# A graph network on one core: edge products copied into the gather ring, and gathers that accumulate onto them

## The chip, the cores and the metric

The kernel runs on one core of one Trainium2 chip. The metric is device time in microseconds (us), the median of several runs. Before the change it is 4117.99 us (three runs, 4102.45 to 4145.95). A profile is one further execution, taken by the hardware profiler.

## What is computed

There are 6250 nodes with 256 features and 100,000 edges with 64 features, sorted by their target `dst`; `src` is random. Two layers follow one another, and each ends in a residual sum and a layer norm:

```python
# layer 0
e = relu((x[dst] - x[src]) @ theta_w.T + theta_b + x[src] @ phi_w.T + phi_b)
x = layernorm(x + segment_max(e, dst))            # 0 where a node has no edge
# layer 1
hv = x @ W_in + b_in
for W, b in ((W_u0, b_u0), (W_u1, b_u1)):
    m = relu(concat([hv[src], he]) @ W + b)       # he: the 64 edge features
    hv = where(has_in, segment_max(m, dst) + hv, hv)
x = layernorm(x + relu(hv @ W_ro + b_ro))
```

So there are three passes over the edges, each a maximum over the edges of a node. Since a product with a row of a table can be taken before the rows are gathered, an edge costs a gathered row of a table of 6250 x 256 numbers; in passes 1 and 2 the product of its own 64 features is added to that row.

## The kernel before

The edges lie in 782 steps of 128 (one on each partition), the steps in 17 blocks: twelve of 56 steps, then 48, 32, 16, 8 and 6. Within a block each partition holds consecutive edges, one a step. Eight steps make a chunk (98 in all). `sweep(r)` (L705) issues one pass in program order; nothing reorders it, each engine takes its instructions as they stand there and waits on semaphores.

For a step `s` the loop at L906 does this:

- `sources` (L716) issues on POOL the indirect gather of step `s + 16` (`AHEAD`): 128 rows of 1 KB of `table[r]`, by the indices `s_s`, into a tile `run` of 8 steps, of which there are 4 (`bufs=4`).
- In passes 1 and 2, `features` (L723) loads a chunk of transposed edge features `hT` from the ACT queue, three chunks early, and `pair` (L727) makes on PE the product `hp` of two steps in one PSUM bank; there are two such banks (`tag="he"`). L923 adds it to the two gathered steps on DVE.
- L926 is the running maximum on DVE: `cur = max(min(prev, lim), cur)`, where `lim` cuts it at a new node.
- After each chunk L932 stores the 1 MB tile to `S` in DRAM from SP's queue.

At the end of a block `over_lanes` (L734) carries the maximum across partitions: PE transposes the last step (`lp`), DVE scans it (`scan`, L746, at the first step after the block), PE turns it back (`back`, L753, one step later), ACT copies it to `cs`.

`node` (L763) finishes 128 nodes, 49 tiles of them in a pass. Its parts are put on steps with `at(slot, f)`. `rows` (L769) gathers on POOL, at step `g`, the last edge's row of each node from `S`; it waits for all stores issued before it. `picks` and `carried` (three and two steps before `b`) bring the carried part `v` into PSUM. From step `b` on comes the arithmetic: `first_a` to `first_i` in pass 0 (relu, residual with `x_sb`, statistics on DVE, square root on ACT, norm, transposes on PE, two products with `wcat`, the next table's rows stored from ACT's queue), `next_a` to `next_d` in pass 1, `next_a` to `next_c` and `last_d` to `last_g` in pass 2. The planner at L896 to L901 sets the steps:

```python
gap = (4, 4, 6)[r]
...
    e = max(FIRST[SPAN[t][1]] + BLOCKS[SPAN[t][1]], begin)
    b = max(b + (gap if b < FS else 3), e + 4, min(e + AHEAD + 4, FS + 4))
    node(t, max(e, b - AHEAD - 4), b)
```

`e` is the end of the last block in which the tile's nodes can end. In pass 0 there are also the counts of edges per node (`count`, L643), from which `end_i`, the indices for `rows`, come, and `theta` (L797), the part of layer 0 that belongs to the target. `x` lies in SBUF (`x_sb`, 49 KB a partition); layer 0's result takes its place there.

Of the kernel before, what the change touches and what calls it, by code (L numbers as in the profile page):

```python
# [17 lines left out]
P = 128  # L18
N = 6250
D = 256  # L20
# [22 lines left out]
KEPT = 7  # L43
# [11 lines left out]
SPAN = [span(t) for t in range(NT)]  # L55

# [377 lines left out]
def gnn_kernel(  # L434
# [6 lines left out]
    table = [dram.tile([ROWS, D], F32, name=f"table{r}") for r in range(3)]  # L441


    jmp = const.tile([P, P], I32)
# [7 lines left out]
    col_i = const.tile([P, P], I32)  # L452
# [97 lines left out]
def in_order(ctx: ExitStack, tc: tile.TileContext, g):  # L550
# [9 lines left out]
    heT, xTn, xn, out = (g[n] for n in ("heT", "xTn", "xn", "out"))  # L560
    ctx.enter_context(tc.manual_schedule())
# [4 lines left out]
    x_sb = one.tile([P, NT, D], F32, name="x_sb")  # L566
# [9 lines left out]
    def weight(w, name):  # L576
        t = one.tile([P, 2, D], F32, name=name)
        nc.scalar.dma_start(t, w.rearrange("(k p) f -> p k f", p=P))
        return t
# [7 lines left out]
    tb, pb = line(g["th_b"], "tb"), line(g["ph_b"], "pb")  # L587
    wcat = one.tile([P, 2, 2 * D], F32, name="wcat")
    nc.scalar.dma_start(wcat[:, :, :D], g["w_in"].rearrange("(k p) f -> p k f", p=P))
    winT = weight(g["w_inT"], "winT")  # L590
    wu0 = weight(g["w_u0"][:D, :], "wu0")
# [51 lines left out]
    def count(c):  # L643
        k = min(K, FS - c * K)
        cut = slice(c * K, c * K + k)
        ol = work.tile([P, K, P], BF16, name="ol", bufs=1)
# [57 lines left out]

    def sweep(r):  # L705
# [10 lines left out]
        def sources(s):  # L716
            if s % K == 0:
                runs[s // K] = work.tile([P, K, D], F32, name="run", bufs=4)
            nc.gpsimd.indirect_dma_start(  # L719
                out=runs[s // K][:, s % K, :], out_offset=None, in_=table[r],  # L720
                in_offset=bass.IndirectOffsetOnAxis(ap=s_s[:, s:s + 1], axis=0))

        def features(c):  # L723
            hT[c] = work.tile([P, K // 2, P], F32, name="hT", bufs=4)
            nc.scalar.dma_start(hT[c].rearrange("p q e -> p (q e)"), heT[c])

        def pair(i):  # L727
            c, q = divmod(i, K // 2)
            hp[i] = psum.tile([P, 512], F32, tag="he", name="hp")
            nc.tensor.matmul(hp[i], hT[c][:, q, :], whe[r - 1].rearrange("p s f -> p (s f)"), start=True, stop=True)  # L730
            if q == K // 2 - 1:
                del hT[c]

        def over_lanes(b, last):  # L734
# [25 lines left out]
            at(FIRST[b] + BLOCKS[b], scan)  # L760
            at(FIRST[b] + BLOCKS[b] + 1, back)

        def node(t, g, b):  # L763
# [22 lines left out]
            def carried():  # L786
                assert max(carried_in) - SPAN[t][0] < KEPT
                o["v"] = psum.tile([P, 512], F32, tag="v", name="v")
                for blk, p in o["pick"]:
                    nc.tensor.matmul(o["v"][:, :N1], p, cs[:, blk % KEPT, :N1], start=(blk == SPAN[t][0]),  # L790
                                     stop=(blk == SPAN[t][1]))

            def x_in():
                o["xT"] = work.tile([P, 2, P], F32, name="xT", bufs=3)
                nc.sync.dma_start(o["xT"], xTn[:, :, t * P:(t + 1) * P])
# [12 lines left out]
            def first_b():  # L808
                nc.vector.tensor_add(o["m"], o["m"], h_sb[:, t, :])
                nc.scalar.activation(o["m"], o["m"], AF.Relu, scale=has[:, t:t + 1])  # L810

            def first_c():
                nc.vector.tensor_add(o["m"], o["m"], x_sb[:, t, :])
# [4 lines left out]
            def first_e():  # L818
                norm(x_sb[:, t, :], o["m"], *o["mv"])
                o["aT"] = turned(x_sb[:, t, :])  # L820

            def first_f():
                o["g"] = times(o["aT"], wcat[:, :, D:], b2, D)

            def first_g():
                o["ps"] = times(o["aT"], wcat[:, :, :D], None, D)

            def first_h():
                new = work.tile([P, D], F32, name="new", bufs=3)
                nc.scalar.copy(new, o["g"][:, :D])  # L830
                nc.scalar.dma_start(table[1][t * P:(t + 1) * P, :], new)

            def first_i():
                nc.scalar.copy(h_sb[:, t, :], o["ps"][:, :D])

            def next_a():
                nc.vector.tensor_max(o["m"], o["m"], o["v"][:, :D])  # L837
                nc.scalar.activation(o["m"], o["m"], AF.Relu, scale=has[:, t:t + 1])
# [8 lines left out]
            def next_d():  # L847
                new = work.tile([P, D], F32, name="new", bufs=3)
# [3 lines left out]
            def last_d():  # L852
                nc.vector.scalar_tensor_tensor(o["m"], o["ps"][:, :D], 0.0, x_sb[:, t, :], OP.max, OP.add)  # L853

            def last_e():
                o["mv"] = stats(o["m"], "m")

            def last_f():
                o["y"] = work.tile([P, D], F32, name="new", bufs=3)
                norm(o["y"], o["m"], *o["mv"])  # L860
# [4 lines left out]
            at(g, rows)  # L865
            if r == 0:
# [3 lines left out]
            at(b - 3, picks)  # L870
            at(b - 2, carried)
            if r == 0:
                for i, f in ((0, first_a), (1, first_b), (3, first_c), (4, first_d), (6, first_e), (7, first_f),
                             (8, first_g), (9, first_h), (10, first_i)):
                    at(b + i, f)
            else:
                for i, f in ((0, next_a), (2, next_b), (3, next_c)):
                    at(b + i, f)
                for i, f in ((5, next_d),) if r == 1 else ((5, last_d), (6, last_e), (8, last_f), (9, last_g)):
# [3 lines left out]
        if r == 0:  # L883
# [4 lines left out]
            for i in range(NT // PART):  # L888
                at(14 + 8 * i, lambda i=i: nc.sync.dma_start(x_sb[:, i * PART:(i + 1) * PART, :],
                                                             xn[:, i * PART:(i + 1) * PART, :]))  # L890
# [5 lines left out]
        gap = (4, 4, 6)[r]  # L896
# [95 lines left out]
```

## Time and profile before

| | |
|---|---|
| median of three runs | 4117.99 us |
| profiled execution | 4091.96 us |
| its span | 4090.2 us |
| mean granted TensorE clock | 0.667 of full |
| first to last gather, passes 0, 1, 2 | 59.8 to 1339.3, 1389.9 to 2664.5, 2710.4 to 4007.4 us |
| read from and written to HBM | 401.01 MB, 333.16 MB |

In the lines of groups a row has source line, engine, operation, what it writes and reads, count, busy time and mean ns of one, then the engine's idle time before it and who ended that. In the answers by stretches the columns are the length, then busy time and number of instructions of PE, its weight loads, DVE, ACT and POOL, then the granted TensorE clock, the mean busy share of the 16 DMA engines and GB/s. A timeline line has the start, the duration, the instruction, and in brackets the idle time before it with its releaser. Releasers are inferred from semaphore events, and some matmul records can be missing.

### The profile page before, as it was taken

To read this page: it belongs to the slowest core of one execution; us is meant where nothing else is said; L and a number is where in the kernel's file an instruction comes from. 1 tells how busy PE (TensorE), PEld (TensorE's weight loads), DVE (VectorE), ACT (ScalarE), POOL (GpSimd) and SP (SyncE) were. 2 spreads that over 40 slices of the span, in tenths; PEclk is the share of its full clock that TensorE was granted. 3 is DMA by queue.
4 is the path that set the end of the run, shared out by engine and by line. 5 is a ranking of instruction groups with operands and counts; after the bars stand their busy time and mean duration, and the time that the engine had idled before them with its cause. 6 is when DMAs were issued, how large, how long until landed. Compare 5 with 4: busy or idle time off the path is not lost.

```text
span 4090.2 us, 22048 instructions
## 1 busy us (share of the span) xinstructions
PE 2032.6 (50%) x4957; PEld 915.2 (22%) x4957; DVE 2083.0 (51%) x4526; ACT 280.7 (7%) x770; POOL 2459.6 (60%) x2499
## 2 busy tenths in 40 slices
PE   5433444232334745455464555664455545555557
PEld 4222222111112311111121222221121212122223
DVE  2766733433334555454554454545555555555555
ACT  1000010000101100000000000110000000000001
POOL 3777755666664466566666655546666666655542
PEclk7555565555555867676777777786766777777766
DMA  6755544454554456565555555545655555555542
GB/s 223 250 195 181 195 157 169 166 181 161 170 168 147 147 189 211 172 205 179 195 192 184 181 181 183 172 164 191 204 191 193 191 180 192 182 174 171 175 146 86
DMA packets 237763, 735.87 MB, mean 180 GB/s; under 512 B 51880, under 2 KB 91799, under 8 KB 200375
## 3 DMA queue, kind: packets, MB, share of 16 engines
q0 software_dynamic: 119664, 326.92, 26.7%
q1 hardware_dynamic: 66096, 334.71, 21.5%
q10 hardware_dynamic: 51862, 72.75, 5.4%
q8 instruction: 42, 0.69, 0.1%
q14 instruction: 99, 0.80, 0.1%
HBM read 401.01 MB, written 333.16 MB: 179 GB/s over the span
## 4 chain that ended last, share of the span: by engine, by line
another core or an unknown queue 31%; DVE 18%; PE 16%; issue 15%; POOL 9%; DMA 8%; ACT 1%; ACTq 0%; DVEq 0%; POOLq 0%; SPq 0%
POOL run L719 9%; DVE run L926 8%; DVE run L923 7%; DMA run<-table,s_s 5%; PE hp L730 5%; PE prod L700 4%; PE prod L702 2%; PE v L790 2%; DMA S<-run 1%; PE ps L533 1%; PE tp L692 1%; ACT aT L694 1%; DVE pick L783 1%; DMA hT<-in_heT 0%
## 5 line engine op out<-in xcount | busy, mean ns | idle before, releaser
L719 POOL DMA_INDIRECT run<-table,s_s x2346 | 2316.6, 987 | 1294.2 <-issue 696.2
L730 PE MATMUL hp<-whe,hT 128*128 128x512 f32 x1564 | 1054.5, 779 | 589.7 <-DVE run L923 378.2
L926 DVE SCALAR_TENSOR_TENSOR run<-run,lim 128x256 f32<-128x256 f32 x2295 | 1110.6, 484 | 205.7 <-DMA run<-table,s_s 120.5
L923 DVE TENSOR_TENSOR run<-run,hp 128x512 f32<-128x512 f32 x782 | 533.7, 682 | 809.0 <-remote 459.7
L730 PEld LDWEIGHTS hp<-whe,hT 128*128 128x128 f32 x1564 | 308.0, 233 | 1190.7 <-DVE run L923 699.6
L771 POOL DMA_INDIRECT m<-S,end_i x147 | 142.4, 969 | 291.6 <-DMA S<-run 191.4
L700 PE MATMUL prod<-wcat,aT 128*128 128x256 f32 x392 | 160.4, 550 | 261.9 <-ACT aT L694 167.6
L790 PE MATMUL v<-cs,pick 128*128 128x256 f32 (+1 forms) x468 | 192.6, 540 | 123.9 <-DVE pick L783 70.9
L692 PE MATMUL tp<-ident,h_sb 128*128 128x128 f32 x196 | 52.7, 361 | 358.9 <-DVE h_sb L841 223.6
L653 PE MATMUL hist<-oh,ol 128*128 128x49 bf16 x782 | 48.8, 217 | 249.2 <-DVE oh L650 182.2
L700 PEld LDWEIGHTS prod<-wcat,aT 128*128 128x128 f32 x392 | 95.5, 268 | 314.2 <-ACT aT L694 177.6
L790 PEld LDWEIGHTS v<-cs,pick 128*128 128x128 f32 x468 | 116.2, 272 | 199.6 <-issue 83.5
L746 DVE TENSOR_TENSOR_SCAN cT<-lim,cT,lp 128x128 f32<-128x128 f32 x96 | 40.8, 468 | 218.5 <-PE lp L741 144.5
L853 DVE SCALAR_TENSOR_TENSOR m<-prod,x_sb 128x256 f32<-128x256 f32 x49 | 20.8, 424 | 248.9 <-remote 169.9
L700 PE MATMUL prod<-wro,aT 128*128 128x256 f32 x196 | 90.4, 609 | 96.8 <-issue 76.1
L647 DVE TENSOR_TENSOR ol<-col,lo 128x1024 bf16<-128x1024 bf16 x98 | 119.3, 1217 | 26.3 <-remote 25.7
L692 PEld LDWEIGHTS tp<-ident,h_sb 128*128 128x128 f32 x196 | 25.1, 173 | 451.4 <-issue 318.5
L741 PE MATMUL lp<-ident,run 128*128 128x128 f32 x102 | 28.7, 375 | 183.0 <-ACT lim L739 101.5
L700 PE MATMUL prod<-wu,aT 128*128 128x256 f32 x196 | 75.6, 524 | 68.4 <-ACT aT L694 36.7
L837 DVE TENSOR_TENSOR m<-m,v 128x256 f32<-128x256 f32 x98 | 40.5, 414 | 134.9 <-remote 78.1
L653 PEld LDWEIGHTS <-ol 128*128 128x128 bf16 x782 | 42.8, 117 | 276.2 <-DVE ol L647 164.5
L700 PE MATMUL prod<-th,xT 128*128 128x256 f32 x196 | 95.5, 640 | 8.8 <-issue 8.8
(116 smaller groups left out, 1326.0 us busy)
## 6 DMA issues: line engine op xcount, KB each, us to landing
S<-run SPq DMA_DIRECT2D x291, 1024.0 KB
hT<-in_heT ACTq DMA_DIRECT2D x196, 256.0 KB
run<-table,s_s POOLq DMA_INDIRECT x2346
table<-new ACTq DMA_DIRECT2D x98, 128.0 KB
xg<-in_xTn SPq DMA_DIRECT2D x7, 896.0 KB
table<-g SPq DMA_DIRECT2D x7, 896.0 KB
xT<-in_xTn SPq DMA_DIRECT2D x49, 128.0 KB
x_sb<-in_xn SPq DMA_DIRECT2D x7, 896.0 KB
```

What stands on the lines that cost most here:

```text
L533: nc.tensor.matmul(ps[:, q * D:(q + 1) * D], xg[:, k, (i + q) * P:(i + q + 1) * P], wd[:, k, :], start=(k == 0), stop=(k == 1))
L647: nc.vector.tensor_tensor(ol[:, :k, :], col.unsqueeze(1).to_broadcast([P, k, P]), lo[:, cut].unsqueeze(2).to_broadcast([P, k, P]), OP.is_e ...
L653: nc.tensor.matmul(hist[:, :NT], ol[:, j, :], oh[:, j, :], start=(c == 0 and j == 0), stop=(c == NG - 1 and j == k - 1))
L692: nc.tensor.transpose(tp[:, k * P:(k + 1) * P], a[:, k * P:(k + 1) * P], ident)
L700: nc.tensor.matmul(ps[:, :n], aT[:, k, :], w[:, k, :], start=(k == 0), stop=(k == 1 and b is None))
L702: nc.tensor.matmul(ps[:, :n], every[0:1, :], b, start=False, stop=True)
L719: nc.gpsimd.indirect_dma_start(out=runs[s // K][:, s % K, :], out_offset=None, in_=table[r], in_offset=bass.IndirectOffsetOnAxis(ap=s_s[:, ...
L730: nc.tensor.matmul(hp[i], hT[c][:, q, :], whe[r - 1].rearrange("p s f -> p (s f)"), start=True, stop=True)
L771: i = nc.gpsimd.indirect_dma_start(out=o["m"], out_offset=None, in_=S_r[:P * (FIRST[SPAN[t][1]] + BLOCKS[SPAN[t][1]]), :], in_offset=bass. ...
L790: nc.tensor.matmul(o["v"][:, :N1], p, cs[:, blk % KEPT, :N1], start=(blk == SPAN[t][0]), stop=(blk == SPAN[t][1]))
L923: nc.vector.tensor_add(two, two, hp.pop(s // 2))
L926: nc.vector.scalar_tensor_tensor(cur, prev, lim[:, s:s + 1], cur, OP.min, OP.max)
```

## The change

The edge products no longer meet the gathered rows on DVE. The ring of `run` tiles grows from 4 to 10 and is shared by the passes. For a chunk of passes 1 and 2, `products` loads `hT` (from SP's queue), makes the four products on PE and lets ACT copy each from PSUM into the ring tile; it is called seven chunks (56 steps) ahead of the step, and for the first seven chunks of a pass during the last four chunks of the pass before. The gather into that tile then has `compute_op` add. Steps ahead for the gathers stay 16.

To make room, `x_sb` goes: rows of `x` are loaded for each tile in pass 0 and rows of layer 0's result, stored to `x1` in DRAM, in pass 2. Some weights that are needed early lie in a tile of the ring. Also: `scan` and `back` run 15 steps later (5 near the end), `v` is copied to SBUF by ACT 17 steps before its use, relu of the nodes moves from ACT to DVE (in the last step of pass 2 the other way), two products with `wcat` become one of 512 columns, and nodes are at least 6 steps apart in all passes.

```diff
-KEPT = 7
+RING = 10
+EARLY = 7
+KEPT = 9
+def calm(s):
+    return 16 if s < FS - 120 else 6
...
+    def products(r, c):
+        hT = work.tile([P, K // 2, P], F32, tag="pt", name="hT", bufs=4)
+        nc.sync.dma_start(hT.rearrange("p q e -> p (q e)"), heT[c])
+        runs[r, c] = work.tile([P, K, D], F32, tag="run", name="run", bufs=RING)
+        for q in range(min(K, FS - c * K) // 2):
+            hp = psum.tile([P, 512], F32, tag="he", name="hp")
+            nc.tensor.matmul(hp, hT[:, q, :], whe[r - 1].rearrange("p s f -> p (s f)"), start=True, stop=True)
+            nc.scalar.copy(runs[r, c][:, 2 * q:2 * q + 2, :].rearrange("p s f -> p (s f)"), hp)
...
             nc.gpsimd.indirect_dma_start(
-                out=runs[s // K][:, s % K, :], out_offset=None, in_=table[r],
-                in_offset=bass.IndirectOffsetOnAxis(ap=s_s[:, s:s + 1], axis=0))
+                out=runs[r, c][:, j, :], out_offset=None, in_=table[r],
+                in_offset=bass.IndirectOffsetOnAxis(ap=s_s[:, s:s + 1], axis=0),
+                **({"compute_op": OP.add} if r > 0 else {}))
...
-            at(FIRST[b] + BLOCKS[b], scan)
-            at(FIRST[b] + BLOCKS[b] + 1, back)
+            e = FIRST[b] + BLOCKS[b]
+            at(e + calm(e) - 1, scan)
+            at(e + calm(e), back)
...
+                o["v"] = work.tile([P, D + 2], F32, name="vs", bufs=4)
+                nc.scalar.copy(o["v"][:, :N1], v[:, :N1])
+            def x_row():
+                o["x"] = work.tile([P, D], F32, name="x", bufs=3)
+                nc.sync.dma_start(o["x"], xn[:, t, :] if r == 0 else x1[t * P:(t + 1) * P, :])
...
-                nc.scalar.activation(o["m"], o["m"], AF.Relu, scale=has[:, t:t + 1])
+                nc.vector.tensor_scalar(o["m"], o["m"], 0.0, has[:, t:t + 1], OP.max, OP.mult)
...
-                norm(x_sb[:, t, :], o["m"], *o["mv"])
-                o["aT"] = turned(x_sb[:, t, :])
+                norm(o["x"], o["m"], *o["mv"])
+                o["aT"] = turned(o["x"])
+                nc.scalar.dma_start(x1[t * P:(t + 1) * P, :], o["x"])
...
-            at(b - 3, picks)
-            at(b - 2, carried)
+            at(b - late - 2, picks)
+            at(b - late - 1, carried)
...
-        gap = (4, 4, 6)[r]
+        gap = 6
...
-            b = max(b + (gap if b < FS else 3), e + 4, min(e + AHEAD + 4, FS + 4))
-            node(t, max(e, b - AHEAD - 4), b)
+            c = calm(e)
+            b = max(b + (gap if b < FS else 3), min(max(e + 2 * c + 4, e + AHEAD + 4), FS + 4))
+            node(t, max(e, b - AHEAD - 4), b, c)
...
-                if s % 2 == 0:
-                    if s + 2 < FS:
-                        pair(s // 2 + 1)
-                    two = runs[c][:, j:j + 2, :].rearrange("p s f -> p (s f)")
-                    nc.vector.tensor_add(two, two, hp.pop(s // 2))
-            cur = runs[c][:, j, :]
+            if j == 0:
+                if r > 0 and c + EARLY < NG:
+                    products(r, c + EARLY)
+                elif r < 2 and c >= NG - 4:
+                    for i in range(2 * (c - NG + 4), min(2 * (c - NG + 5), EARLY)):
+                        products(r + 1, i)
+            cur = runs[r, c][:, j, :]
```

## Prediction, on record before the change was measured

> **What bounds the kernel now.** I read the page first, then busy time by stretches, the timeline of one stretch, and the waits of POOL. The stretches are cut at the first and last gather of each pass; between them lie the lead-in, the turn to the next pass (passes 0 to 1: 50.6 us, 1 to 2: 45.9 us) and the tail.
>
> ```profile
> PE 2032.6 (50%) x4957; PEld 915.2 (22%) x4957; DVE 2083.0 (51%) x4526; ACT 280.7 (7%) x770; POOL 2459.6 (60%) x2499
> q0 software_dynamic: 119664, 326.92, 26.7%
> q1 hardware_dynamic: 66096, 334.71, 21.5%
> q10 hardware_dynamic: 51862, 72.75, 5.4%
> another core or an unknown queue 31%; DVE 18%; PE 16%; issue 15%; POOL 9%; DMA 8%; ACT 1%; ACTq 0%; DVEq 0%; POOLq 0%; SPq 0%
> L719 POOL DMA_INDIRECT run<-table,s_s x2346 | 2316.6, 987 | 1294.2 <-issue 696.2
> L926 DVE SCALAR_TENSOR_TENSOR run<-run,lim 128x256 f32<-128x256 f32 x2295 | 1110.6, 484 | 205.7 <-DMA run<-table,s_s 120.5
> L923 DVE TENSOR_TENSOR run<-run,hp 128x512 f32<-128x512 f32 x782 | 533.7, 682 | 809.0 <-remote 459.7
> ```
>
> No engine is full on this page, and nearly a third of the chain has no name. The stretches (POOL is the last engine column) give the floor:
>
> ```profile
> 59.80:1339.30 1279.50, 467.77 (x1777) 280.70 (x1778) 624.63 (x1383) 103.72 (x296) 845.02 (x827) 0.54 0.53 179
> 1389.90:2664.50 1274.60, 684.88 (x1297) 252.69 (x1297) 658.21 (x1317) 62.19 (x164) 801.90 (x826) 0.72 0.57 188
> 2710.40:4007.40 1297.00, 701.52 (x1267) 263.35 (x1268) 698.41 (x1488) 56.66 (x157) 797.05 (x825) 0.71 0.55 184
> ```
>
> POOL's timeline shows 0.30 us between any two gathers, so an issue costs 1.25 us, not 0.95. Busy time plus 0.30 per instruction makes 1093 of 1279.5 us in pass 0, 1050 of 1274.6 in pass 1, 1045 of 1297.0 in pass 2. What POOL stands still is 186, 225 and 252 us: 663 us, the most that can be won while a gather costs POOL what it does.
>
> Why it stands still is on DVE's timeline, in pass 1:
>
> ```profile
> 1443.99 0.69 DVE L923 TENSOR_TENSOR run<-run,hp 128x512 f32<-128x512 f32 x1 [3.87 <-issue]
> 1448.90 0.69 DVE L923 TENSOR_TENSOR run<-run,hp 128x512 f32<-128x512 f32 x1 [3.18 <-DMA run<-table,s_s]
> 1454.49 0.69 DVE L923 TENSOR_TENSOR run<-run,hp 128x512 f32<-128x512 f32 x1 [3.86 <-remote]
> ...
> 1511.92 0.68 DVE L923 TENSOR_TENSOR run<-run,hp 128x512 f32<-128x512 f32 x1
> 1513.56 0.68 DVE L923 TENSOR_TENSOR run<-run,hp 128x512 f32<-128x512 f32 x1
> ```
>
> The adds of two steps come 5.5 us apart (10 in 55.3 us, granted clock 0.50), then 1.64 us apart (clock 1.00). The three releasers named for the slow ones differ, and none can be true: by 1494.6 us POOL had issued 80 gathers and DVE had made 27 adds, 54 steps, so the rows lay there 26 steps ahead. What is late is the edge product, whose matmul records end too early or are missing. Run back to back at speed, a product takes PE 1.37 us (four in 5.46 us at 1505.06). So in slow stretches PE gives a product per 5.5 us, 2.8 us a step, more than twice POOL's pace; DVE has only the two PSUM buffers as stock; the ring of 4 chunks fills, and POOL stops:
>
> ```profile
> POOL run L719 <- DVE run L926: 77.4, 15, 14.9
> POOL run L719 <- DMA S<-run: 76.1, 10, 13.9
> POOL run L719 <- DVE run L923: 31.3, 8, 11.0
> ```
>
> Two of its halts: 3.64 us before 1484.67, 11.61 before 1506.11. Pass 0 has no edge products, but DVE waits there for transposes of the lanes (cT from lp: 135.4 us in 11 waits) and for picks (no: 93.7 and 49.6 us), PE again.
>
> **What the skill says.** "TensorE: Matmul & The Clock Gate", Part 1: an idle array falls to half clock after a window of some 3.4 us and comes back after a busy one; a caveat reports it stuck at a quarter for 50 us and more. The trace agrees with the caveat in size: 5.5 against 1.37 us is a factor of 4, at a recorded 0.50. "DMA: Bandwidth & Descriptors", SWDGE vs HWDGE: accumulating is for GpSimd's software path only, and one copy is a pair of descriptors; Rules for kernel authors: the accumulate reads its destination and writes it later. It gives no price, and no accumulating gather is in this trace. "ScalarE: Activation LUTs", What ACT_TABLE_LOAD costs: 186 ns + 0.833 ns per element for an instruction with immediates, 612 ns for 512; the trace has 586 ns for such a copy (g from ps, L536), which I use.
>
> **The change part by part.**
>
> *Adds off DVE.* 391 x 0.682 = 267 us a pass leave DVE; its scan, 0.484 us a step, then needs 379 us of a pass. DVE follows the rows and no longer sets the pace: no time by itself, but a DVE held up by late products is what filled the ring.
>
> *Products into the ring.* PE makes the same 391 products a pass. ACT gets 391 x 0.586 = 229 us a pass, and 49 copies of v at about 0.37 us = 18 us; it has 62 and 57 us of busy time now, so it has room. Its order does not: copies of products lie ahead of node work, and with PE at 5.5 us a product, the four of a chunk hold ACT 22 us. Pass 0 has no products, and in pass 1 the node's DVE work takes nothing late from ACT; in pass 2 the norm waits for the square root two steps (2.5 us) after its statistics. Cover gone, DVE stalls there, and rows waits with it; I leave 5 us for it beyond pass 1.
>
> *Slack.* Each gather of passes 1 and 2 now waits for its copy; behind it in POOL's queue stand all later gathers and the rows gathers, and DVE waits for both. PE may now be 56 steps ahead of DVE; gathers are issued up to 16, so some 40 steps are stock. In a slow stretch PE loses 1/1.25 - 1/2.8 = 0.44 step per us, so the stock lasts about 90 us, against 55 and 40 us of the two slow stretches that I read (1443.9 to 1499.2, 1544 to 1584); at speed it gains about 1/0.69 - 1/1.25 = 0.65, less the node matmuls. Most halts should be covered, not all: node matmuls slow down as well, and PE works in bursts that may let the clock fall oftener. I leave 105 of 225 us in pass 1, 110 of 252 in pass 2.
>
> *Lanes and nodes.* Moving scan and back 15 steps later (5 near the end) and v 17 steps ahead, into SBUF, takes DVE's waits for lp and v away: 135 + 94 + 50 us of DVE in pass 0. POOL meets them only through the rows gathers and the ring (its waits there: m for S 88 us, run for lp 34 and for DVE 27). I halve its 186: 93 stay. A ring of 10 chunks is part of this. The gap of 6 slots instead of 4 puts one node more behind the last step (7 for 6) in passes 0 and 1: under 5 us.
>
> *Moved DMAs.* 196 loads of hT go from ACT's queue to SP's, 7 chunks early; SP waits there for stores in order, which follow DVE, so they have 60 us of cover. x rows: 49 loads of 128 KB for 7 of 896 KB, the same bytes; x1 adds 49 stores on ACT (0.33 us each) and 49 loads in pass 2: 12.8 MB of 736. Nothing. Relu on DVE (0.42 for ACT's 0.51), one 512-wide product for two: nothing.
>
> *The accumulating gather.* The unknown. POOL: below nothing is excluded, since it does all it does now; zero is the low end. High end: a third descriptor for two, half of 0.97 us again. I take 0.05 us, for the extra wait on ACT's copies: 782 x 0.05 = 39 us a pass. DMA: a gather takes 26.7% x 4090.2 / 2493 = 0.44 us of each of the 16 engines, the rest (26.9% over 2346 steps) 0.47 a step. Doubled (read two, write one) a step needs 1.35 us of engine time, and the busiest stretch shown runs at 0.89. That is at POOL's pace; [...] I take it as just covered.
>
> *Sum, on the profiled span.* Lead-in 60 + pass 0 (1093 + 93 = 1186) + turn 51 + pass 1 (1050 + 39 + 105 = 1194) + turn 46 + pass 2 (1045 + 39 + 110 = 1194) + tail 83 = 3814 us against 4090. The profiled execution took 4091.96 us, 26 below the median 4117.99; so 3840 for the median.
>
> **Rivals.**
>
> (a) *POOL pays for the accumulate* (slower). With 0.48 us more an issue, a pass is 1050 + 375 + 20 = 1445; in all 4316, median 4342. It decides from about 0.05 + 276/1564 = 0.23 us an issue, a little later since longer issues also give PE time. For: software writes the descriptors. Against: 0.95 us may be mostly fixed. 0.14.
>
> (b) *DMA saturates* (slower). At three times the engine time a step needs 1.79 us: 1400 us a pass at full share; with POOL's other stalls none, 3 x as above gives about 4225, median 4250, more at 0.89. Breaks even near 2.2 to 2.5 times. For: 0.89 is already seen. Against: the mean is 0.55. 0.13.
>
> (c) *Slow PE remains the bound.* Bursts keep it slow; the stock only delays halts. Passes 1 and 2 keep 200 us each of stillness, 185 more than in my sum: 4025 in the median. For: the clock stood at 0.50 in each stretch of 10 us from 1440 to 1500, under steady demand. Against: the halts of POOL come only when a stock of 2 products is gone. 0.20, of which three quarters are still over 1% below before.
>
> (d) *All halts go.* Pass 1093, 1060, 1060: 3453 with the rest, median 3480 to 3600. 0.08.
>
> Mine: 0.45, own range 3620 to 3960. Together faster by over 1% (under 4077) 0.68, within 1%, about what a measurement here can tell, 0.05, slower 0.27. The range 3540 to 4370 leaves out half of (d) and the far ends of (a) and (b).
>
> **What would show it.** Right: L719 at about 1.0 us and 0.30 gap in passes 1 and 2, POOL still 210 us there together, ACT near 300 us a pass, no DVE wait of 3 us on products. (a): L719 over 1.2 us. (b): DMA share near 0.9 in passes 1 and 2, POOL waiting for landings. (c): POOL waits for ACT's copies, clock 0.50 in long stretches. The forecast fails if a gather's price rises by over 0.2 us, or if PE's slow stretches outlast 90 us or halts come back as soon as they end.

## The result, and the profile after

The changed kernel takes 4552.82 us (median of 4 runs, 4535.99 to 4555.76), the kernel before beside it 4110.22 (4095.35 to 4145.95): 1.105 times, interval 1.098 to 1.113. It is slower; the forecast was 3840, with 4370 as the upper end of its range. Where the runs of one kernel spread, a ratio here uses those within 1.5% of its fastest.

From the page of the changed kernel: busy time of the engines, the queue of the gathers, the gather (now L744), the scan (L946) and ACT's copy of a product (L727):

```profile
PE 2037.2 (45%) x4761; PEld 925.5 (20%) x4761; DVE 1643.8 (36%) x3891; ACT 723.5 (16%) x1601; POOL 3391.2 (74%) x2499
q0 software_dynamic: 269808, 326.92, 40.6%
L744 POOL DMA_INDIRECT run<-table,s_s x2346 | 3244.0, 1383 | 854.4 <-issue 632.4
L946 DVE SCALAR_TENSOR_TENSOR run<-run,lim 128x256 f32<-128x256 f32 x2295 | 1107.7, 483 | 2259.6 <-DMA run<-table,s_s 2043.9
L727 ACT COPY run<-hp 128x512 f32<-128x512 f32 x782 | 458.6, 586 | 2126.5 <-PE hp L726 1938.3
```

DVE lost its 439 us and ACT gained its 443, as planned; POOL gained 932 us with the same 2499 instructions. The mean gather went from 987 to 1383 ns, although the 782 gathers of pass 0 are unchanged. Queue q0 moves the same 326.92 MB in 269808 packets instead of 119664. DVE now waits 2044 us for rows.

The same three stretches as before (columns: from and to, length, PE, weight loads, DVE, ACT, POOL, granted clock, DMA share, GB/s):

```profile
58.70:1361.00 1302.30, 468.55 (x1612) 236.29 (x1613) 628.36 (x1405) 99.97 (x293) 850.50 (x825) 0.55 0.54 179
1444.20:2953.60 1509.40, 707.15 (x1310) 295.82 (x1309) 437.70 (x988) 279.77 (x557) 1258.30 (x825) 0.70 0.76 160
2991.70:4506.90 1515.20, 689.18 (x1263) 290.05 (x1262) 489.60 (x1188) 275.09 (x573) 1264.12 (x825) 0.69 0.76 161
```

In pass 1, 1258.3 us of busy time and 825 gaps of 0.305 us (252) make 1510: POOL never stands still. POOL's timeline at the start of pass 1 (start, duration, what it is, idle time before it) shows where its time goes, and one long wait in the turn ahead of it:

```profile
1444.22 1.59 POOL L744 DMA_INDIRECT run<-table,s_s  x1 [37.19 <-ACT run L727]
1446.12 1.56 POOL L744 DMA_INDIRECT run<-table,s_s  x1 [0.30 <-issue]
```

An accumulating gather costs POOL 1.55 us (median) where a plain one costs 0.946, with the same gap. Set against the sum of the prediction: passes 1 and 2 together 3025 us for 2388 (+637), pass 0 1302 for 1186 (+116), the turns 83 and 38 for 51 and 46 (+24), the tail 46 for 83 (-37), in all +739, which is 4553 less 3814 (the lead-in is 1 us shorter).

Pass 0 has no accumulating gather and still did not gain. Its stillness (idle time of POOL over 0.5 us before an instruction, counted so from here on) is 204 us, against 189 before. POOL's waits there, and then DVE's (total, times, longest):

```profile
POOL m L787 <- DMA S<-run: 129.8, 7, 31.7
```

```profile
DVE sd L698 <- ACT sd L694: 154.2, 18, 32.5
```

The halts on the ring are gone and have become halts of the rows gathers, which wait for stores of S. Those wait for DVE, and DVE waits in order for a square root that stands on ACT behind a copy of a late product of PE (theta, `h_sb` from `prod`). The longest of these waits:

```profile
708.81 0.37 ACT L823 COPY h_sb<-prod 128x256 f32<-128x256 f32 x1 [15.13 <-remote]
709.41 0.16 DVE L698 RECIPROCAL sd<-sd 128x1 f32<-128x1 f32 x1 [32.51 <-ACT sd L694]
```

The copy needs nothing but that product. PE's own record of it ends at 683.4, 25 us before. Profiles of the same pass 0 in later runs took 1254 to 1281 us (e1, e3, e4, e9, e11), so part of the +116 is scatter.

### The profile page after: what moved, and what is told of

The parts are those of the page before. It is cut to its first block, busy times and chain, and to the rows that moved or that the text cites. A ratio compares the mean times of both kernels' runs of the same rounds, so it can differ in the third digit from the quotient of the medians.

```text
span 4553.4 us, 23306 instructions
## 1 busy us (share of the span) xinstructions
PE 2037.2 (45%) x4761; PEld 925.5 (20%) x4761; DVE 1643.8 (36%) x3891; ACT 723.5 (16%) x1601; POOL 3391.2 (74%) x2499
## 3 DMA queue, kind: packets, MB, share of 16 engines
q0 software_dynamic: 269808, 326.92, 40.6%
## 4 chain that ended last, share of the span: by engine, by line
DMA 24%; issue 18%; POOL 17%; PE 12%; DVE 3%; another core or an unknown queue 3%; ACT 2%; SPq 1%; ACTq 0%; POOLq 0%; DVEq 0%
POOL run L744 16%; DMA run<-table,s_s 12%; DMA hT<-in_heT 11%; PE hp L726 9%; DVE run L946 2%; ACT run L727 1%; PE prod L712 1%; PE prod L848 1%; PE v L806 1%; SPq L952 0%; PE prod L714 0%; DMA m<-S,end_i 0%; POOL m L787 0%; ACT aT L706 0%
## 5 line engine op out<-in xcount | busy, mean ns | idle before, releaser
L744 POOL DMA_INDIRECT run<-table,s_s x2346 | 3244.0, 1383 | 854.4 <-issue 632.4
L946 DVE SCALAR_TENSOR_TENSOR run<-run,lim 128x256 f32<-128x256 f32 x2295 | 1107.7, 483 | 2259.6 <-DMA run<-table,s_s 2043.9
L726 PE MATMUL hp<-whe,hT 128*128 128x512 f32 x1564 | 1142.2, 897 | 1419.9 <-DMA hT<-in_heT 1407.3
L726 PEld LDWEIGHTS hp<-whe,hT 128*128 128x128 f32 x1564 | 425.6, 291 | 2075.1 <-issue 1206.3
L727 ACT COPY run<-hp 128x512 f32<-128x512 f32 x782 | 458.6, 586 | 2126.5 <-PE hp L726 1938.3
L848 PE MATMUL prod<-wcat,aT 128*128 128x512 f32 x196 | 152.2, 920 | 68.7 <-issue 45.3
L665 PE MATMUL hist<-oh,ol 128*128 128x49 bf16 x782 | 48.9, 217 | 236.0 <-DVE oh L662 174.2
L704 PE MATMUL tp<-ident,x 128*128 128x128 f32 x98 | 29.0, 393 | 233.5 <-DVE x L699 99.0
L809 ACT COPY vs<-v 128x256 f32<-128x256 f32 (+1 forms) x147 | 55.0, 374 | 321.0 <-PE v L806 176.3
L706 ACT COPY aT<-tp 128x256 f32<-128x256 f32 x147 | 55.0, 374 | 229.3 <-PE tp L704 117.6
L848 PEld LDWEIGHTS prod<-wcat,aT 128*128 128x128 f32 x196 | 50.2, 282 | 128.8 <-issue 95.3
L712 PE MATMUL prod<-wro,aT 128*128 128x256 f32 x196 | 65.6, 465 | 23.6 <-ACT aT L706 20.3
```

The lines of the kernel that those rows point to most:

```text
L665: nc.tensor.matmul(hist[:, :NT], ol[:, j, :], oh[:, j, :], start=(c == 0 and j == 0), stop=(c == NG - 1 and j == k - 1))
L704: nc.tensor.transpose(tp[:, k * P:(k + 1) * P], a[:, k * P:(k + 1) * P], ident)
L706: nc.scalar.copy(aT.rearrange("p k e -> p (k e)"), tp[:, :2 * P])
L712: nc.tensor.matmul(ps[:, :n], aT[:, k, :], w[:, k, :], start=(k == 0), stop=(k == 1 and b is None))
L726: nc.tensor.matmul(hp, hT[:, q, :], whe[r - 1].rearrange("p s f -> p (s f)"), start=True, stop=True)
L727: nc.scalar.copy(runs[r, c][:, 2 * q:2 * q + 2, :].rearrange("p s f -> p (s f)"), hp)
```

## The experiments

Three questions: what an accumulating gather costs, whether the rest of the change is worth something, and what the late products hang on. A product is called late here when ACT's copy of it starts at least 1.9 us after that of the product before it in the same chunk; there are 293 such distances in a pass. The runs came from several chips. On four of them the kernel before took 4098 to 4133 us (medians), on one 3417, so ratios are always to the kernel before on the same chip. The one trace of the kernel before is from the first measurement.

### The price of the accumulate

**e1_plain_gather**: the changed kernel without the accumulate.

```diff
-                in_offset=bass.IndirectOffsetOnAxis(ap=s_s[:, s:s + 1], axis=0),
-                **({"compute_op": OP.add} if r > 0 else {}))
+                in_offset=bass.IndirectOffsetOnAxis(ap=s_s[:, s:s + 1], axis=0))
```

> The changed kernel with the add taken off the gathers of passes 1 and 2; rows overwrite the copied products, so the edge features are left out of the result. Everything else stays: ACT's copies, the waits of the gathers on them, the ring of 10, pass 0. Theory (the price of the accumulate on POOL is the whole loss): an issue goes back from 1.55 to 0.95 us, POOL does not stand still in passes 1 and 2, each takes 1050 to 1100 us instead of 1510, and the whole is 4553 less 2 x 430 = about 3690 us. Rival (slow TensorE only looks solved because POOL became slow): stillness of POOL of 150 us or more a pass comes back, passes of 1200 us and more, 3930 us or more. Rival (the engines' DMA time is the limit): passes stay above 1300 us.

Measured: 4344.81 us, 1.063 times before (1.050 to 1.075). The issue is back at 946 ns, and stillness is back with it: 249 us in pass 1 and 460 in pass 2, where the changed kernel had none. Late products are back too: 87 and 82 of 293, where the changed kernel had none. The rival of the slow TensorE was right. The change makes the kernel 10.5% slower, and without the accumulate it is still 6.3% slower: what the cheaper issue gives back is in large part lost again to the stillness that returns.

**e3_rows64** and **e4_bytes512** change the size of a gather, with the accumulate in pass 1 and without it in pass 2 (e4 gathers from `table` seen as twice as many rows of half the length). Passes 1 and 2 of e3, then of e4:

```diff
...
+                    out=runs[r, c][:P // 2, j, :], out_offset=None, in_=table[r],
+                    in_offset=bass.IndirectOffsetOnAxis(ap=s_s[:P // 2, s:s + 1], axis=0),
+                    **({"compute_op": OP.add} if r == 1 else {}))
```

```diff
...
+                    out=runs[r, c][:, j, :D // 2], out_offset=None,
+                    in_=table[r].rearrange("n (h f) -> (n h) f", h=2),
+                    in_offset=bass.IndirectOffsetOnAxis(ap=s_s[:, s:s + 1], axis=0),
+                    **({"compute_op": OP.add} if r == 1 else {}))
```

> Prices inside one kernel. The changed kernel, but in pass 1 the accumulating gathers fetch 64 rows instead of 128 and in pass 2 the gathers fetch 64 rows without accumulating (half of the rows are left out, and in pass 2 the products too). Theory (POOL pays for each row's descriptors): accumulating 128 rows costs 1.55 us and 64 rows about half of the part above a fixed cost, so 0.9 us or less; plain goes from 0.95 to about 0.6 us. Rival (a fixed charge of 0.6 us for any accumulate, say another code path or wait): 64 rows accumulating cost 0.6 us more than 64 rows plain.

> Prices inside one kernel. The changed kernel, but each gather of pass 1 accumulates 128 rows of 512 B instead of 1 KB, each of pass 2 gathers 128 rows of 512 B without accumulating (half of each row is left out, and rows are taken from half-row places). Theory (descriptors are the price): issues stay at 1.55 and 0.95 us. Rival (bytes are the price, because POOL waits for its descriptors to be drained): the accumulating issue falls toward 1.25 us and the plain one below 0.95.

Measured (medians of an issue): 64 rows 1.422 us accumulating, 0.900 plain; half the bytes 1.550 and 0.947; the full gather 1.550 and 0.946. Halving the rows takes the surcharge from 0.604 to 0.522 us, much nearer to the rival of e3 than to its theory; halving the bytes leaves it at 0.603, as the theory of e4 said. So most of it is a charge per instruction. Late products in the same two runs: 1 of 293 in each accumulating pass, 86 and 89 in the plain ones. So neither half the rows nor half the bytes makes PE come in time.

### Order on ACT, and a chip without late products

In **e6_plain_root** and **e7_after_root** the square roots leave ACT; e6 is otherwise e1, e7 the changed kernel.

```diff
-        nc.scalar.activation(sd, mv[:, 1:2], AF.Sqrt, bias=eps)
+        hv, q = (work.tile([P, 1], F32, name=i) for i in ("hv", "q"))
+        nc.vector.tensor_scalar(sd, mv[:, 1:2], EPS, None, OP.add)
+        nc.vector.tensor_scalar(hv, sd, -0.5, None, OP.mult)
+        bits = sd.bitcast(I32)
+        nc.vector.tensor_scalar(bits, bits, 1, None, OP.arith_shift_right)
+        nc.vector.tensor_scalar(bits, bits, -1.0, float(0x5F3759DF), OP.mult, OP.add)
+        for _ in range(2):
+            nc.vector.tensor_mul(q, sd, sd)
+            nc.vector.tensor_scalar(q, q, hv, 1.5, OP.mult, OP.add)
+            nc.vector.tensor_mul(sd, sd, q)
...
-        nc.vector.reciprocal(sd, sd)
```

> Plain gathers (the products are overwritten and left out of the sum), and the square root of both norms worked out on DVE (a guess from the bits and two Newton steps, 10 small instructions in place of ACT's root and the reciprocal) instead of on ACT, so that DVE no longer waits for an instruction that stands behind ACT's copies. Theory, DVE was held by ACT's order: the 424 us that DVE waited for roots in pass 2 go, pass 2 falls from 1497 to 1250-1330 us, pass 0 from 1272 to 1150-1220, and the whole from 4345 to 4000-4150. Rival, the root was only where the lateness of PE's products showed first and the wait moves to the next thing that PE or ACT owes (v, cT, transposes): pass 2 stays over 1420, pass 0 over 1240, the whole over 4230.

> The changed kernel with nothing else than the square roots on DVE (as in e6). Theory (ACT's order is what kept pass 0 from gaining): pass 0 falls from 1302 to 1170-1230 us; passes 1 and 2 stay at 1509 and 1515 +- 10 us, since GpSimd is full there whatever DVE and ACT do; the whole 4440-4490. Rival (pass 0 waits for PE, by whatever road): pass 0 1270-1310, the whole 4520-4570.

They ran on the chip where the kernel before takes 3417 us (12 runs, 3395 to 3427). Measured: e6 3435.19, 1.007 times before (1.005 to 1.010), e7 4350.44 (one run), 1.27 times. Neither has a late product or any stillness in its three passes, so on the roots these two runs say nothing. Pass 0 of e7 took 1106 us; the same pass with ACT's roots, in e5 below on the same chip, took 1104, also without stillness. The two do give the accumulate alone, everything else equal. Pass 1 of e6, then of e7:

```profile
1228.10:2277.20 1049.10, 654.51 (x1297) 276.16 (x1295) 432.99 (x981) 275.68 (x551) 798.07 (x825) 0.77 0.68 230
```

```profile
1228.10:2735.60 1507.50, 697.28 (x1309) 293.15 (x1308) 437.76 (x988) 279.22 (x556) 1256.13 (x825) 0.70 0.75 160
```

458.4 us over 782 gathers, 0.586 us each (0.584 in pass 2). It also shows the changed work at its floor: 1049 us is the 1050 that the prediction took for POOL without stillness.

**e10_plain_root_again** is e6, on a chip where products come late.

> The kernel of e6_plain_root again (plain gathers, products left out of the sum, square roots on DVE). On a chip without late products: within 1.5% of before, GpSimd never still. On a chip with them, where the same kernel with ACT's roots took 1.063 times before (e1): theory (ACT's order turned late products into DVE's waits for roots) gives 0.97 to 1.02 times before, with pass 2 at 1250 to 1330 us and pass 0 at 1150 to 1230; rival (the wait moves to the next thing PE owes) 1.04 to 1.07, pass 2 over 1420.

Measured: 4268.80, 1.034 times before (1.028 to 1.041), between the two theories. Pass 2 went to 1355 us with 311 of stillness (e1: 1497 and 460; e9 below, with ACT's roots on the same chip as e10: 1511 and 470). Pass 0 gained nothing: 1309 us against e9's 1267. DVE's waits in pass 2, of e1 and then of e10:

```profile
DVE sd L698 <- ACT sd L694: 423.7, 22, 52.7
```

```profile
DVE new L887 <- ACT new L884: 127.3, 18, 30.0
DVE cT L768 <- PE hp L734: 70.7, 2, 52.2
DVE m L867 <- ACT vs L816: 58.5, 7, 20.9
```

The 424 us behind the root go; other things that PE and ACT owe take part of their place (relu's result, the lanes' transposes, v). ACT's order cost some 150 us of pass 2 (one profile each), not the rest.

**e11_after_again** is the changed kernel as it is, on the chip of e10.

> The changed kernel itself, beside before and the others on one chip. If full GpSimd (2 x 782 x 1.855 us in passes 1 and 2) is what sets its time, its passes 1 and 2 last 1505 to 1520 us on any chip, with and without late products; only pass 0 and the turns differ: 4340 to 4380 us on a chip without late products (1.27 times before, pass 0 at about 1105 us), 4540 to 4570 with them (1.10 to 1.11 times). If late products still cost something in passes 1 and 2, those passes would be over 15 us shorter on a chip without them.

Measured: 4534.92, 1.099 (1.090 to 1.107); passes 1 and 2 1508.8 and 1511.6 us. On the chip of the result they took 1509 and 1515, on the chip without late products (e7) 1507.5 and 1510.9. Whether or not products come late on a chip, these passes differ by less than 5 us, as the theory said: POOL alone sets them. The whole came out 5 us below the forecast range.

### What the late products hang on

**e5_paced**: plain gathers, but in pass 1 POOL does idle work after each.

```diff
+        fill = work.tile([P, 2 * P], F32, tag="xT", name="fill", bufs=2) if r == 1 else None
...
+            if r == 1:
+                for i in range(2):
+                    nc.gpsimd.memset(fill, 0.0)
```

> Plain gathers (no accumulate) in all passes, so the products written into the ring are overwritten by the rows and left out of the sum; in pass 1 alone GpSimd also writes 128x256 zeros twice after each gather, so that its gathers come about as far apart as accumulating ones did (1.85 us). Question: is it the slower pace of the accumulating gathers that kept PE's edge products from coming 5.6 us apart, or the kind of transfer? Theory, the pace: in pass 1 fewer than 5 of some 380 distances between products are at or over 5 us (69 of 367 with plain gathers at full pace), and GpSimd stands still under 30 us; pass 1 then lasts 782 x 1.85 = about 1450 us. Rival, the kind of transfer: 40 to 75 distances of 5 us or more stay in pass 1. Pass 2, not paced, keeps some 70 of them in either case and lasts 1497 +- 40 us.

Measured: 4005.12, on the chip without late products: none in either pass, so the question stayed open, and the run was made again elsewhere.

**e9_paced_again**

> The kernel of e5_paced again (plain gathers, products left out of the sum, two memsets of GpSimd after each gather of pass 1 alone), since on the chip of e5 no product at all came late, with or without the pacing. Where a chip makes products late (unpaced pass 2 has 70 or more of its 293 distances inside a chunk at or over 1.9 us): theory, the pace keeps PE fast: under 5 in pass 1; rival, the accumulating transfer itself did: 60 to 100 in pass 1 too. Where the chip makes none late in pass 2 (as in e5): zero in pass 1 as well, about 4005 us, and the question stays open.

Measured: 4623.94. In pass 1 the gathers came 1.93 us apart on average (1591 us less 30 of stillness and 43 rows gathers at 1.28, over 782): no late product of 293. In pass 2, at full pace, 89 of 293, and 470 us of stillness. That the two passes differ in other work does not explain it: pass 1 of e10, at full pace on the same chip, has 100 of 293. ACT's timeline of this one kernel, a chunk of pass 1 and then one of pass 2; the first column is the start of each copy:

```profile
2002.85 0.58 ACT L727 COPY run<-hp 128x512 f32<-128x512 f32 x1 [10.47 <-PE hp L726]
2004.56 0.58 ACT L727 COPY run<-hp 128x512 f32<-128x512 f32 x1 [1.12 <-PE hp L726]
2005.55 0.58 ACT L727 COPY run<-hp 128x512 f32<-128x512 f32 x1 [0.41 <-PE hp L726]
2006.41 0.58 ACT L727 COPY run<-hp 128x512 f32<-128x512 f32 x1 [0.27 <-PE hp L726]
```

```profile
3493.23 0.59 ACT L727 COPY run<-hp 128x512 f32<-128x512 f32 x1 [4.52 <-remote]
3498.13 0.58 ACT L727 COPY run<-hp 128x512 f32<-128x512 f32 x1 [4.31 <-remote]
3503.03 0.58 ACT L727 COPY run<-hp 128x512 f32<-128x512 f32 x1 [4.32 <-remote]
3509.32 0.58 ACT L727 COPY run<-hp 128x512 f32<-128x512 f32 x1 [5.71 <-issue]
```

Four products come 1.71, 0.99 and 0.86 us apart in the first, 4.90, 4.90 and 6.29 in the second. In two stretches of this kernel (columns as before), the recorded clock is 0.50 both within the 1.71 and over all of the second chunk:

```profile
2003.00:2004.00 1.00, 1.00 (x2) 0.31 (x1) 0.00 (x0) 0.44 (x1) 0.84 (x2) 0.50 0.41 131
3493.00:3512.00 19.00, 8.26 (x8) 2.00 (x8) 0.00 (x0) 2.34 (x4) 14.43 (x16) 0.50 0.36 106
```

The pace of POOL's gathers decides it, not the accumulate: the theory was right. So the changed kernel's fast PE was a by-product of its slow gathers.

**e13_before_pace64, e14_before_pace128, e16_before_pace256** take the kernel before and do nothing but slow its gathers down, in all passes (64, 128 or 256 elements):

```diff
+    fill = one.tile([P, 64], F32, name="fill")
...
+            nc.gpsimd.memset(fill, 0.0)
```

> The kernel before, full result, with one GpSimd memset of 128x64 after every gather of all three passes and nothing else; it should cost about 0.1 us a gather (estimate: 128x256 took 0.319 us), so gathers come about 1.35 us apart instead of 1.25. Theory A (the late products go with a slightly slower pace already): no distance inside a chunk over 1.9 us for reasons of PE, GpSimd stands still under 60 us a pass, the passes last 1130 to 1200 us and the whole 3600 to 3750 against about 4110. Theory B (they go only at a much slower pace, as the 2.0 us tried): products stay late, stillness absorbs the fillers, the whole is 4030 to 4200. On a chip without late products at all (before about 3417): 3600 to 3680 in both cases.

> As e13 with memsets of 128x128 (about 0.17 us each by the same estimate, gathers about 1.42 us apart). Theory A: GpSimd stands still under 40 us a pass, passes of 1190 to 1260 us, the whole 3780 to 3900. Theory B (still too fast a pace): 4080 to 4250. Pass 0 by itself: if its stillness (186 us) has the same cause as the late products, it falls below 40 us here whenever passes 1 and 2 do; if not, it stays at 120 to 190 us. On a chip without late products: 3780 to 3860.

> The kernel before, full result, with a memset of 128x256 (0.319 us in e5) after each gather of all passes: a pace of about 1.46 us. A step at this pace alone gives passes of about 1205 to 1250 us. Theory (stillness goes on falling by 170 us for each 0.1 us of pace): 200 to 260 us are left of 400, the whole is 3950 to 4030 (0.955 to 0.975 times before). Rival (what is left is stillness of another cause, so pacing now only adds): stillness stays over 350 us and the whole is over 4090.

| kernel | mean us from gather to gather in pass 1, without stillness and rows gathers | stillness in passes 0, 1, 2 (us) | times before |
| --- | --- | --- | --- |
| before | 1.26 | 189, 231, 260 | 1 |
| e13 | 1.31 | 123, 215, 233 | 0.987 (0.982 to 0.992) |
| e14 | 1.36 | 68, 176, 157 | 0.976 (0.971 to 0.981) |
| e16 | 1.48 | 2, 4, 5 | 0.943 (0.936 to 0.949) |

The memsets took 0.167, 0.221 and 0.330 us. e13 (4078.96 us) and e14 (4032.52) came out as theory B said or a little better. e16 (3874.70) went beyond its theory. A fall of stillness alone proves little, since a memset also fills time in which POOL would have waited: beyond the gap that they fill, the memsets add some 30, 75 and 160 us of work a pass, and in pass 1 stillness fell by 16, 56 and 227. What does tell is how far the gathers are ahead when DVE adds. In pass 1 of the kernel before they are 13 steps ahead (median), and 455 us of the waits before these adds fall where four or more steps of rows lie ahead, so that the product is what is missing. In e13 it is 405 us, in e14 362, in e16 only 67, and there the gathers are 2 steps ahead: DVE now waits for rows, as its releasers also say, and most of the lateness goes between 1.36 and 1.48 us. The rows of e16 on its page (busy time, mean ns, idle time before), and that wait (total, times, longest):

```profile
L721 POOL DMA_INDIRECT run<-table,s_s x2346 | 2345.9, 1000 | 528.3 <-issue 400.2
L724 POOL MEMSET fill<- 128x256 f32 x2346 | 773.5, 330 | 1.3
DVE run L926 <- DMA run<-table,s_s: 422.3, 234, 11.8
```

774 us of work that nobody needs, and 240 us less in all, against 4115.39 of the kernel before on its chip. Part of a memset falls into the gap that POOL has anyway: the gaps of up to 0.5 us add up to 143 us a pass in e16 and 240 to 245 before. The rest pays for itself out of the stillness. Pass 0, which has no edge products, loses its stillness too, and the chip without late products has none in it (1104 us in e5, with the code of the changed kernel). So its cause hangs on the pace and on the chip like that of the others; that it is the same is likely and not shown. Neither deeper stock nor moved lanes nor moved roots helped there.

### Versions

**e2_two_rings**: the products are copied 40 steps ahead to a ring of their own, the gathers are plain, and DVE adds, as before; the rest of the change stays. **e8** and **e12** add the roots on DVE, **e15** and **e18** a memset of 128x64 or 128x160 after each gather of passes 1 and 2.

```diff
-RING = 10
-EARLY = 7
+RING = 4
+MADE = 6
+EARLY = 5
...
+            if r > 0 and j % 2 == 0:
+                two = runs[r, c][:, j:j + 2, :].rearrange("p s f -> p (s f)")
+                nc.vector.tensor_add(two, two, made[r, c][:, j:j + 2, :].rearrange("p s f -> p (s f)"))
```

> The whole result is computed. The changed kernel, but ACT copies the products into a ring of their own (6 chunks, 5 ahead), gathers are plain into a ring of 4 chunks, and DVE adds the two from SBUF, two steps at a time. Theory: POOL issues at 0.95 us, DVE has about 770 us of work a pass and room for it, PE's products come in bursts ahead of need; passes 1 and 2 take 1060 to 1150 us each and the whole about 3700 to 3850 us, faster than both kernels by 6 to 10%. Rival (taking the add off DVE was what mattered): DVE waits in order for late work of the nodes, the ring of 4 fills, POOL stands still 150 us or more a pass, 4000 us or more.

> The products 40 steps ahead in a ring of their own, plain gathers, DVE adds (as e2_two_rings, full result), and the square roots on DVE. Theory: e2 lost 117 us in pass 0 and 133 + 118 us in pass 2 to DVE's waits for roots; about half of that was GpSimd's stillness, so pass 0 falls from 1242 to 1170-1210, pass 2 from 1294 to 1190-1250, pass 1 stays at 1260 +- 25, and the whole goes from 4037 to 3850-3950. Rival (the waits move on): the whole stays over 3990.

> The kernel of e8_two_rings_root again (two rings, DVE adds, plain gathers, roots on DVE). On a chip with late products, where e2 took 0.983 times before: theory 0.93 to 0.97, pass 2 at 1180 to 1250 us; rival (the waits move on) 0.97 to 0.99. On a chip without them: 1.03 to 1.05 as in e8, from gathers whose issues take longer on GpSimd while DVE adds, and longer turns.

> The two-ring version with roots on DVE (e8, e12; full result, plain gathers, DVE adds), and a GpSimd memset of 128x64 after each gather of passes 1 and 2. e12 took 0.986 times before, with 157, 182 and 128 us of stillness. Theory A: in passes 1 and 2 stillness falls below 40 us, the passes last 1180 to 1230 us, the whole is 0.94 to 0.97 times before. Theory B: stillness stays over 100 us in each, the whole 0.98 to 1.01. On a chip without late products: 1.06 to 1.09.

> The two-ring version with roots on DVE and a memset of 128x160 (about 0.25 us) instead of 128x64 (0.169) after each gather of passes 1 and 2. e15 had 84 and 119 us of stillness there and took 0.971 times before. Theory (stillness goes on falling): under 60 us in each of the two passes, 0.955 to 0.975 times before. Rival (past the lowest point): stillness falls by less than the 65 us a pass that the pacing adds, 0.98 to 1.00.

Measured, in times before: e2 0.983 (0.972 to 0.994; 4037.17 us), e12 0.986 (0.982 to 0.989), e15 0.971 (0.966 to 0.976), e18 0.963 (0.955 to 0.971; 3948.99 us). On the chip without late products, e8 1.039 (1.035 to 1.044; 3545.47 us). Stillness in passes 0, 1, 2: e2 143, 148, 192; e12 158, 182, 129; e15 173, 84, 119; e18 175, 17, 18. In e2 and e12 the rivals were right, in e15 the time came to the edge of theory A's and the stillness did not, in e18 both were the theory's. e2's stillness in passes 0 and 1 lies a little under the 150 us that its rival named, and e8 can't decide between its theory and its rival, which were written for late products. e12's 19 runs spread from 4029.73 to 4126.22 us and only seven of them enter its ratio; the median of all, 4103.24, is 0.995 times before. So the change with stock in front of DVE instead of the accumulate gains about 1.7% where products are late (e2); what of it the stock gives, no run isolates. The roots on DVE add nothing to it that shows (another chip, overlapping intervals).

Pacing adds more, and late products first become less late and then fewer: 77 and 61 of 293 in passes 1 and 2 of e12 (gathers 1.25 us apart, median), 82 and 88 in e15 (1.29), 28 and 40 in e18 (1.37), of which 41 and 23, 3 and 2, and none are 5 us or more. Pacing alone, without any of the change (e16), is the fastest of all on those chips. It is ahead of e18, on the same chip, by what e18 leaves unpaced: passes 1 and 2 of e18 are the shorter ones (1195 and 1200 us against 1219 each), but pass 0 takes 1275 against 1243, and the turns and the tail 78 us more. Pacing all passes of the two-ring version was not tried.

## Why the prediction was wrong

**The accumulating gather** is the step that failed first. It took "0.05 us, for the extra wait on ACT's copies"; measured are 0.586 us (e7 against e6) to 0.604, mostly per instruction. Its high end, half of 0.97 us, was still too low. The term 39 us a pass should have been 458. With the prediction's own 1050 that alone gives 1508 a pass; measured are 1509 and 1515. Its 105 and 110 us of stillness did not come, which hides part of the miss: twice 419 us, less 215, is 623 of the +637. Why POOL takes longer is open. What the instruction makes shows in the queue: 144 packets instead of 48 (150144 more over 1564 gathers is 96 each). Rival (a) named the mechanism, its sign (an issue over 1.2 us) and its breaking point (0.23 us an issue). Its price was 0.12 too low and its pass 0 too good, hence 4342. The prediction's other term for this instruction, the doubled time of the DMA engines, was right: the queue's 48.9% of pass 1, less 43 rows gathers at 0.44 us, is 0.92 us of each engine for a gather.

**Slack** failed as well, and e1 shows it once the first failure is taken away: not 105 and 110 us of stillness were left but 249 and 460. Rival (c) was right on this: the stock only delays the halts. Its sign, POOL waiting for ACT's copies, did not come: in pass 2 of e1 425 of the 460 us lie in front of rows gathers, 9 at such copies. What was wrong is the picture of a slow stretch as something given, which lasts so long and can be outlasted. It goes on while gathers keep their pace. A larger stock in front of POOL would let the gathers run on, and so the slow PE too. That last link is an inference; shown is that slower gathers end the lateness (e9, e16) and the stillness (e16). In the changed kernel the slow gathers did it, so no stillness at all was left in passes 1 and 2.

**Products into the ring**: the busy time was right (ACT 280 and 275 us against "near 300"). The 5 us left for the square root in pass 2 were not: DVE waited 424 us for it in e1, and moving it took stillness in pass 2 from 470 to 311 us (e9 to e10).

**Lanes and nodes**: halving pass 0's 186 us failed. The waits named (lp, v) did go; the stores took their place, and stillness stayed at 204. That stillness goes away with slower gathers (e14, e16) and is absent on one chip (e5), as in the other passes.

**Adds off DVE**: right, and worth no time that shows (e6 is 1.007 times before on the chip without late products). **Moved DMAs**: "nothing" was not right for the turns. The one to pass 1 grew by 33 us and the next shrank by 8. The first gather's wait of 37 us is put down to a copy by ACT, but that copy, at 1443.23, belongs to a later chunk, and the seven chunks copied ahead were done by 1400. The last rows of the new table were stored from 1441.62 on, and the gather followed at 1444.22, 2.6 us later; before the change it followed the last store by 2.5 us. So it waits for the table, which the nodes finish later; no run isolates why. Rival (b), DMA at its limit, is excluded: the share was 0.76 while POOL waited for nothing. (By the prediction's own figures its break-even lies at 2.4 to 2.8 times, not 2.2 to 2.5.)

The Trainium skill, "TensorE: Matmul & The Clock Gate", Part 1, has recorded clock values of a half and of the whole only, and warns in a caveat that such records can't be fully trusted. This case agrees with both: only 0.50 and 1.00 are recorded, and at a recorded 0.50 products come 1.71 us apart in one chunk of e9 and 4.9 to 6.3 in another. The record does not tell late from merely half as fast. One reading of the prediction fails by the same chunk. Its 1.37 us for a product "at speed" was taken where the mean recorded clock was 0.59; where it is 1.00 products come 0.86 us apart (e9). The late ones there are then 5.7 to 7.3 times slower, not 4, and the agreement with the caveat's quarter falls away.

Open: why the gathers' pace does this to PE, and why one chip of five shows none of it. No run separates POOL's own work from the rate of its transfers; half the bytes and half the rows at full pace did not help, which speaks against the amount of data alone. e16 was not run on the chip without late products. There POOL would be full too, so its passes should last about what they do here (1243, 1219, 1219) and the whole near 3870 against 3417, 13% slower; that is an estimate.

## What to carry to other kernels

Before an accumulating gather replaces a plain one, price it on the queue that issues it: here every issue went from 0.95 to 1.55 us, and an engine with 18% of a pass free cannot carry 36% more. When an engine is held up by another that is slow in stretches, ask what switches the slowness on before building stock against it; slowing the suspect with idle work costs a line or two and can answer it. And try a kernel on more than one chip where its stillness has no name: this one's differed by 17% between chips, and what gains a little on one can lose on another (e12 and e8 are one kernel: 0.986 and 1.039).

## What the runs showed that was not expected

- An accumulating gather makes 144 packets where a plain one makes 48, for the same bytes, and costs 0.58 to 0.60 us more to issue; half the rows cost 0.52 more, half the bytes 0.60.
- Useless memsets of 0.33 us after each gather made the kernel before 5.7% faster on a chip with late products.
- POOL leaves 0.305 us between gathers, and a memset between them partly fills that gap: small gaps fell from 240 to 143 us a pass.
- A plain gather's mean issue is 966 ns in pass 1 of e6, where DVE has no adds, and 1040 in e8, where DVE adds two tiles of SBUF; the medians are equal (946). The two kernels differ in their rings too, so that the adds cause it is not shown.
- The plain gather's packets on the queue have a mean of 2732 bytes; the accumulating gathers bring 200192 packets under 2 KB beyond those of e1, which is 128 each, one for a row.
